# Layer 1's logits, masks and left sums on sixteen 32x32 tiles of TensorE, with the masks loaded per step and row group

## The chip, the cores and the metric

The kernel runs on one core of a Trainium2 chip. The metric is the device time of one execution in microseconds (us). The kernel before takes 3537.9 us (median of three runs, 3537.0 to 3539.0).

## The reference

Two graph layers run one after the other on 4096 nodes with 512 features. Both take the same adjacency matrix `adj` (4096 x 4096), of which under 2% is not zero. Layer 0 is full attention with `adj` added twice to the logits. Layer 1, where the change is, has 8 heads of 64 and masked logits that are a sum of two vectors:

```
h  = relu(layernorm(x));  nX = standardized (h @ W) per head           # 8 x 4096 x 64
kg = at1[:, :, None] + at2[:, None, :]                                 # logits of every pair
kg = leaky_relu(kg, 0.2) * adj
mg = where(adj != 0, kg, -32768);  attention = softmax(mg)
x  = x + elu(attention @ nX + nX)
```

## The kernel before, in words

**Layer 0** runs over 256 tiles of 128 sources by 512 rows. Beside its own work each tile of `adj` leaves two things for layer 1 (`for_layer_1`, L707 to L716): the mask `ng` (bf16, 0 where there is an edge, a large negative number where there is none), stored in the DRAM tensor `nT_d` (L715), and the weights `gs` (f32), stored in `gT_d` (L716).

**Layer 1** has 512 steps, `STEPS`. A step is one chunk of 512 rows (`ic`, 8 of them), one group of four heads (`hg`, 2) and one tile of 128 sources (`jt`, 32). 32 steps with the same rows and heads make a group, so there are 16 groups. Every step passes through these functions, in several steps' distance:

- `left_sums(n+1)` on TensorE writes logits of heads 0 and 2 into the PSUM tile `l` (two buffers). It multiplies `z2` (a source's six bf16 parts for each of four heads, in rows 0, 32, 64 and 96 and after) by `z1_left`, a copy of `z1` in which only heads 0 and 2 are not zero. Four matmuls of 64 x 64 (L1075).
- `left_relu(n+1)` on ScalarE applies relu times four in place (L1081).
- `sums(n)` on TensorE adds, for heads 1 and 3 into the PSUM tiles `r0` and `r1` (one buffer each) and for heads 0 and 2 onto `l`, first the logits (`z_product`, four matmuls with 6 rows and 128 columns, L1065) and then the mask, as a product with the identity (eight matmuls of 64 x 64, L1095). [...]
- `right_leaky(n)` on VectorE (L1113, two instructions) makes heads 1 and 3 out of `r1` and `r0`; `right_weigh(n)` on GpSimd (L1119) multiplies them by `g`; `left_weigh(n)` on VectorE (L1122) multiplies `l` by `g` and so frees its buffer.
- `exponent(n-2)` on ScalarE (L1126) takes all four heads.
- `values(n-4)` on TensorE (L1134, f32) adds attention times values to the PSUM tile `accs`.

The program keeps its written order on every engine (`seq`). The loop at the end of `fast_path` writes it: in step n TensorE gets `sums(n)`, `left_sums(n+1)` and the two halves of `values(n-4)`. All loads are issued by SP, in order. Every fourth step `load_adj` fetches `z2`, `nb`, the two halves of `nx` and `g` for the next four steps (L1009, L1013, L1019, L1024). Each has two buffers. When a group's values are complete, `finish` copies `accs` (ScalarE L1187, VectorE L1188) and spreads the rest over later steps: four turns to rows on TensorE (L1198) with a division on VectorE (L1210, L1211), additions by GpSimd's DMA queue, and the store. At that place `exponent(n-2)` is issued in two halves of two heads, one ahead of the copies and one behind. Before layer 1 starts, SP loads `xns` (L1309): four loads of 256 KB one after the other, one for each group of 32 partitions.

Of the kernel before, what the change touches and what calls it, by code (L numbers as in the profile page):

```python
# [11 lines left out]
BF16 = mybir.dt.bfloat16  # L12
# [67 lines left out]
def fast_path(  # L80
# [67 lines left out]
    nT_d = dram.tile([NB, P, N], BF16, name="nT_d")  # L148
# [177 lines left out]
    with tc.tile_pool(name="rows_in", bufs=2) as rows_in, tc.tile_pool(  # L326
# [357 lines left out]
        with tc.tile_pool(name="turns", bufs=6) as turns, tc.tile_pool(  # L684
# [23 lines left out]
            def for_layer_1(s):  # L708
                ic, jt = TILES[s]
                aT = turned[s] if s >= SB else firsts[s]  # L710
                ng = work.tile([P, GC], BF16, name="ng", tag="ng", bufs=2)
                seq(nc.vector.tensor_scalar(ng, aT, 0.0, NEG_BIG, ALU.is_equal, ALU.mult))
                gs = work.tile([P, GC], F32, name="gs", tag="gs", bufs=2)
                seq(nc.vector.scalar_tensor_tensor(gs, ng, G_MASKED / NEG_BIG, aT, ALU.mult, ALU.add))  # L714
                nc.sync.dma_start(out=nT_d[jt, :, ts(ic, GC)], in_=ng)  # L715
                nc.sync.dma_start(out=gT_d[jt, :, ts(ic, GC)], in_=gs)  # L716
# [271 lines left out]
    with tc.tile_pool(name="ga_g", bufs=2) as adjs, tc.tile_pool(  # L988
# [13 lines left out]
        z1_lefts = [gat.tile([P, GC], BF16, name=f"z1_left{k}") for k in range(2)]  # L1002
        for z in z1_lefts:
            seq(nc.vector.memset(z, 0.0))

        def load_adj(q):
            ic, _, jt = STEPS[q * JB]
            z2 = inputs.tile([P, JB * P], BF16, name="z2", tag="z2", bufs=2)
            seq(nc.sync.dma_start(  # L1009
                out=z2, in_=z2_d[:, STEPS[q * JB][1], jt * P : (jt + JB) * P]  # L1010
            ))
            ng = inputs.tile([P, JB, GC], BF16, name="nb", tag="nb", bufs=2)
            seq(nc.sync.dma_start(  # L1013
                out=ng, in_=nT_d[jt : jt + JB, :, ts(ic, GC)].rearrange("t p i -> p t i")
            ))

            nx = inputs.tile([P, JB, GC], BF16, name="nx", tag="nx", bufs=2)
            for r in range(2):
                seq(nc.sync.dma_start(  # L1019
                    out=nx[ts(r, HD)],  # L1020
                    in_=nT_d[jt : jt + JB, ts(1 - r, HD), ts(ic, GC)].rearrange("t p i -> p t i"),
                ))
            g = adjs.tile([P, JB, GC], F32, name="g", tag="g", bufs=2)
            seq(nc.sync.dma_start(  # L1024
                out=g, in_=gT_d[jt : jt + JB, :, ts(ic, GC)].rearrange("t p i -> p t i")
            ))
            loads[q] = (g, (ng, nx), z2)
# [5 lines left out]
        def open_group(n, queue):  # L1033

            ic, hg, _ = STEPS[n]
            z1_left = z1_lefts[(2 * ic + hg) % 2]
            for first in (0, HD):
                rows = slice(first, first + 6)
                seq(queue.dma_start(out=z1_left[rows, :], in_=z1_d[rows, hg, ts(ic, GC)]))
# [3 lines left out]
            groups[ic, hg] = {"z1": z1, "z1_left": z1_left, "u4": u4}  # L1043
# [17 lines left out]
        def z_product(n, hh, out, start):  # L1061

            ic, hg, jt = STEPS[n]
            rows = slice(32 * hh, 32 * hh + 6)
            seq(nc.tensor.matmul(  # L1065
                out, loads[n // JB][2][rows, ts(jt % JB, P)], groups[ic, hg]["z1"][rows, :],
                start=bool(start), stop=False, skip_group_check=not start,
            ))

        def left_sums(n):  # L1070

            lefts[n] = psum.tile([P, 2, GC], F32, name="l", tag="l", bufs=2)
            ic, hg, jt = STEPS[n]
            for r, c in ((0, 0), (1, 1), (0, 1), (1, 0)):
                seq(nc.tensor.matmul(  # L1075
                    lefts[n][ts(c, HD), r, :], loads[n // JB][2][ts(r, HD), jt % JB * P + c * HD :][:, :HD],
                    groups[ic, hg]["z1_left"][ts(r, HD), :], start=True, stop=True,
                ))
# [4 lines left out]
        def sums(n):  # L1083

            jt = STEPS[n][2]
# [3 lines left out]
            for hh in (1, 3, 0, 2):  # L1089
                z_product(n, hh, out[hh], hh % 2)  # L1090
            masks = loads[n // JB][1]
            for first in (1, 0):
                for r, c in ((0, 0), (1, 1), (0, 1), (1, 0)):
                    rows = ts(r, HD)
                    seq(nc.tensor.matmul(  # L1095
                        out[first + 2 * r][ts(c, HD), :], ident_b[rows, rows],
                        masks[r != c][rows, jt % JB, :], start=False, stop=True,
                        skip_group_check=first == 0,
                    ))
            rights[n] = right  # L1100

        def both_heads(n):
            return loads[n // JB][0][:, STEPS[n][2] % JB, :].unsqueeze(1).to_broadcast([P, 2, GC])
# [390 lines left out]
        at_block(14, load_adj, 0)  # L1494
        for ic in range(2):
            load_normalized(ic)
# [39 lines left out]
        for n in range(n_steps + 4):  # L1536
# [12 lines left out]
            if n % JB == 0 and q < n_steps // JB:  # L1549
                load_adj(q)  # L1550
# [31 lines left out]
            if done and STEPS[n - 4][2] == NB - 1:  # L1582
                if ready:
                    exponent(n - 2, slice(0, 2))
                finish(n, *STEPS[n - 4][:2])
                if ready:
                    exponent(n - 2, slice(2, 4))
# [407 lines left out]
```

## Time and profile before

| | us |
|---|---|
| median of three runs | 3537.9 |
| the profiled execution | 3538.4 |
| its span | 3536.6 |
| TensorE busy in it | 3492.0 |
| GpSimd busy | 2285.6 |
| VectorE busy | 2574.3 |
| ScalarE busy | 1771.1 |
| layer 1's matmuls of the values (L1134), 4096 of 0.605 | 1003.0 (they overlap) |
| ScalarE's exponents (L1126), 527 | 976.5 |
| from one group's start to the next in layer 1 | 98.4 |

The profile is of one execution. "Busy" is the union of an engine's instructions; matmuls overlap, so a busy TensorE isn't one at its peak. The page's line of DMA shares says how much of the time the core's 16 DMA engines were occupied, and the line below it how many GB/s they moved; the two need not go together. The chain of waits is followed back from the last instruction to what released each. A stretch of the profile is given by its start and end in us from the start of the span.

### The profile page before, as it was taken

Reading aid. Unit: us, or ns where it says so; the run is one execution under the profiler, and the core shown is the slowest. Engines: PE = TensorE matmul, PEld = TensorE weight load, DVE = VectorE, ACT = ScalarE, POOL = GpSimd, SP = SyncE. Lnnn points to the kernel's source line nnn. Section 1 sums busy time; section 2 is a strip of 40 time slices with the busy share of each in tenths; the row PEclk is TensorE's granted clock in tenths of the full one; section 3 lists DMA queues with packets and bytes.
Section 4 is the critical chain, followed back from the end, with each engine's and each line's share of the span. In section 5 each row is a group of like instructions: output and inputs, shape, how many; then the busy total and the mean of one; then the engine's idle time right before and its main releaser. Section 6 shows DMA issues by size and latency. Waiting matters only on the chain.

```text
span 3536.6 us, 59808 instructions
## 1 busy us (share of the span) xinstructions
PE 3492.0 (99%) x21898; PEld 2149.6 (61%) x21898; DVE 2574.3 (73%) x4262; ACT 1771.1 (50%) x1580; POOL 2285.6 (65%) x1863
## 2 busy tenths in 40 slices
PE   9999999999999999999999999999999999999998
PEld 7888888888888888888887223223222323232232
DVE  6765665656565666656567888888888888888887
ACT  2100111111111111111133999999999999999997
POOL 6754444444444444444567888788888888888886
PEclk9999999999999999999999999999999999999999
DMA  6688888888888888888768777787778877777885
GB/s 226 219 247 246 233 232 250 234 244 247 235 246 247 231 252 241 237 248 232 235 135 183 210 207 204 205 208 214 211 209 219 214 215 206 198 209 209 214 213 147
DMA packets 633550, 779.07 MB, mean 220 GB/s; under 512 B 78560, under 2 KB 461216, under 8 KB 624032
## 3 DMA queue, kind: packets, MB, share of 16 engines
q1 hardware_dynamic: 615680, 742.34, 73.5%
q0 software_dynamic: 16464, 31.98, 5.3%
q8 instruction: 174, 2.85, 0.3%
q10 hardware_dynamic: 1104, 0.85, 0.1%
q14 instruction: 128, 1.05, 0.1%
HBM read 592.97 MB, written 174.19 MB: 217 GB/s over the span
## 4 chain that ended last, share of the span: by engine, by line
PE 90%; DVE 7%; ACT 1%; DMA 1%; issue 1%; SPq 0%; DVEq 0%; ACTq 0%
PE accs L1134 25%; PE XZ L722 21%; PE M L777 20%; PE r L1095 4%; PE r L1065 4%; PE l L1075 3%; PE X L508 3%; PE l L1095 3%; PE Z L508 2%; DVE t L1122 2%; PE y L1327 1%; PE pt L1198 1%; DVE x L837 1%; DVE y L1211 1%; PE accs L1327 1%
## 5 line engine op out<-in xcount | busy, mean ns | idle before, releaser
L1119 POOL TENSOR_TENSOR t<-t,g 128x1024 f32<-128x1024 f32 x512 | 1225.6, 2406 | 268.9 <-DVE t L1113 233.3
L1134 PE MATMUL accs<-t,nX 128*64 128x512 f32 x4096 | 1003.0, 605 | 4.6 <-DVE ob L1188 4.6
L1126 ACT ACTIVATE t<-t 128x2048 f32<-128x2048 f32 (+1 forms) x527 | 976.5, 1853 | 0.2 <-POOL t L1119 0.2
L1113 DVE SCALAR_TENSOR_TENSOR t<-u,at2m,r 128x512 f32<-128x512 f32 x1024 | 719.3, 744 | 194.2 <-issue 152.0
L738 ACT ACTIVATE aT<-aT 128x512 f32<-128x512 f32 x256 | 161.2, 630 | 1387.3 <-DVE aT L734 1387.3
L734 DVE TENSOR_TENSOR aT<-aT,XZ 128x256 f32<-128x256 f32 x884 | 348.7, 418 | 575.1 <-PE XZ L722 570.8
L1122 DVE TENSOR_TENSOR t<-l,g 128x1024 f32<-128x1024 f32 x512 | 623.4, 1218 | 0.0
L1081 ACT ACTIVATE l<-l 128x1024 f32<-128x1024 f32 x512 | 516.3, 1008 | 117.5 <-PE l L1075 66.2
L1134 PEld LDWEIGHTS accs<-t,nX 128*64 128x64 f32 x4096 | 246.5, 136 | 461.9 <-issue 449.5
L722 PE MATMUL XZ<-qt,hS 128*128 128x256 f32 x2024 | 479.1, 379 | 1.0
L750 POOL TENSOR_TENSOR S<-aT 128x256 f32<-128x256 f32 x128 | 93.5, 731 | 506.9 <-ACT aT L738 506.9
L722 PEld LDWEIGHTS XZ<-qt,hS 128*128 128x128 f32 x2024 | 383.9, 190 | 55.9 <-DVE aT L734 4.0
L722 PE MATMUL XZ<-qt,hT 128*128 128x256 f32 x1520 | 369.5, 379 | 0.0
L762 POOL TENSOR_TENSOR total<-total,aT 128x256 f32<-128x256 f32 x360 | 323.0, 910 | 9.4
L722 PEld LDWEIGHTS XZ<-qt,hT 128*128 128x128 f32 x1520 | 288.8, 190 | 39.3
L1065 PEld LDWEIGHTS <-z 6*128 6x128 bf16 x2048 | 52.4, 91 | 422.2 <-DVE t L1113 353.8
L751 POOL TENSOR_TENSOR aT<-aT 128x256 f32<-128x256 f32 x128 | 93.6, 731 | 284.1 <-ACT aT L738 284.0
L777 PE MATMUL M<-tv,aT 128*128 128x256 f32 x1024 | 262.6, 379 | 0.0
L777 PE MATMUL M<-v,aT 128*128 128x256 f32 x1024 | 262.6, 379 | 0.0
L777 PE MATMUL M<-v,S 128*128 128x256 f32 x1024 | 242.5, 380 | 0.0
L714 DVE SCALAR_TENSOR_TENSOR gs<-ng,aT 128x512 f32<-128x512 bf16 x252 | 222.7, 884 | 8.7
L777 PEld LDWEIGHTS M<-v,aT 128*128 128x128 f32 x1024 | 194.6, 190 | 26.5
(267 smaller groups left out, 4552.4 us busy)
## 6 DMA issues: line engine op xcount, KB each, us to landing
g<-gT_d SPq DMA_DIRECT2D x128, 1024.0 KB
ag<-in_adj_dram SPq DMA_DIRECT2D x256, 256.0 KB
hS<-s_d SPq DMA_DIRECT2D x64, 1024.0 KB
gT_d<-gs SPq DMA_DIRECT2D x256, 256.0 KB
nb<-nT_d SPq DMA_DIRECT2D x128, 512.0 KB
nx<-nT_d SPq DMA_DIRECT2D x256, 256.0 KB
hT<-h_d SPq DMA_DIRECT2D x64, 768.0 KB
tv<-vt_d SPq DMA_DIRECT2D x128, 384.0 KB
```

The costliest lines, as they stand in the source:

```text
L714: seq(nc.vector.scalar_tensor_tensor(gs, ng, G_MASKED / NEG_BIG, aT, ALU.mult, ALU.add))
L722: seq(nc.tensor.matmul(out, a, b, start=start and k == 0, stop=k == 1, skip_group_check=not start,))
L734: seq(nc.vector.tensor_add(p, before, part))
L762: seq(nc.gpsimd.tensor_add(t, t, a))
L777: seq(nc.tensor.matmul(sums[ic][i][:, u, :], a[:, ts(u, P)], b, start=jt == 0 and u == 0, stop=jt == NB - 2, skip_group_check=u == 1,))
L1081: seq(nc.scalar.activation(lefts[n], lefts[n], AF.Relu, scale=4.0))
L1095: seq(nc.tensor.matmul(out[first + 2 * r][ts(c, HD), :], ident_b[rows, rows], masks[r != c][rows, jt % JB, :], start=False, stop=True, ski ...
L1113: seq(nc.vector.scalar_tensor_tensor(t[:, 2 + e, :], u4[:, e, :], at2m[:, jt, h : h + 1], right[e], ALU.max, ALU.add))
L1119: seq(nc.gpsimd.tensor_mul(t[:, 2:4, :], t[:, 2:4, :], both_heads(n)))
L1122: seq(nc.vector.tensor_mul(logits[n][:, 0:2, :], lefts.pop(n), both_heads(n)))
L1126: seq(nc.scalar.activation(t, t, AF.Exp))
L1134: seq(nc.tensor.matmul(accs[ts(e, HD), hf, :], nX[jt // SB][:, jt % SB, hg * HG + 2 * hf + e, :], t[:, hf + 2 * e, :], start=jt == 0, stop ...
```

## The change

The masks of a tile are stored in another order, 32 source rows to a block. A step's masks are then loaded into a tile of their own, three steps ahead: four loads, each of the same 128 KB, one into each group of 32 partitions. So each of the four heads has all 128 sources of the mask on its own 32 partitions. `nb` (now with four buffers of one step), `nx` and `z1_left` in their old form are gone. Logits, masks and left sums are written as 32-column matmuls, four to a head: 16 logits, 16 masks and 8 left sums per step. `load_g` is split off and runs one step later than `load_adj`. At a group's end the copies come first and the exponent follows whole.

```diff
-    nT_d = dram.tile([NB, P, N], BF16, name="nT_d")
+    nT_d = dram.tile([NB, NI, R, SB, GC], BF16, name="nT_d")
...
-                nc.sync.dma_start(out=nT_d[jt, :, ts(ic, GC)], in_=ng)
+                nc.sync.dma_start(out=nT_d[jt, ic].rearrange("p c i -> c p i"), in_=ng)
...
-        z1_lefts = [gat.tile([P, GC], BF16, name=f"z1_left{k}") for k in range(2)]
-        for z in z1_lefts:
-            seq(nc.vector.memset(z, 0.0))
...
-            ng = inputs.tile([P, JB, GC], BF16, name="nb", tag="nb", bufs=2)
...
-            nx = inputs.tile([P, JB, GC], BF16, name="nx", tag="nx", bufs=2)
...
+            loads[q] = {"z2": z2}
+
+        def load_g(q):
+            ic, _, jt = STEPS[q * JB]
             g = adjs.tile([P, JB, GC], F32, name="g", tag="g", bufs=2)
...
+        def load_masks(n):
+
+            ic, _, jt = STEPS[n]
+            masks[n] = inputs.tile([P, SB, GC], BF16, name="nb", tag="nb", bufs=4)
+            for r in range(SB):
+                seq(nc.sync.dma_start(out=masks[n][ts(r, R)], in_=nT_d[jt, ic]))
...
+        def z_products(n, hh, out, **flags):
 
             ic, hg, jt = STEPS[n]
-            rows = slice(32 * hh, 32 * hh + 6)
...
+            rows = slice(R * hh, R * hh + 6)
+            for c in range(SB):
+                seq(nc.tensor.matmul(
+                    out[ts(c, R), :], loads[n // JB]["z2"][rows, jt % JB * P + c * R :][:, :R],
+                    groups[ic, hg]["z1"][rows, :], **flags,
+                ))
 
         def left_sums(n):
 
             lefts[n] = psum.tile([P, 2, GC], F32, name="l", tag="l", bufs=2)
...
+            for r in range(2):
+                z_products(n, 2 * r, lefts[n][:, r, :], start=True, stop=True)
...
+            order = (1, 3, 0, 2)
+            for hh in order:
+                right_one = hh % 2 == 1
+                z_products(n, hh, out[hh], start=right_one, stop=False, skip_group_check=not right_one)
+            for hh in order:
+                rows = ts(hh, R)
+                for c in range(SB):
                     seq(nc.tensor.matmul(
-                        out[first + 2 * r][ts(c, HD), :], ident_b[rows, rows],
-                        masks[r != c][rows, jt % JB, :], start=False, stop=True,
-                        skip_group_check=first == 0,
+                        out[hh][ts(c, R), :], ident_b[rows, rows], masks[n][rows, c, :],
+                        start=False, stop=True, skip_group_check=hh % 2 == 0,
                     ))
...
         at_block(14, load_adj, 0)
+        at_block(14, load_g, 0)
+        for n in range(3):
+            at_block(14, load_masks, n)
...
-            if n % JB == 0 and q < n_steps // JB:
-                load_adj(q)
+            if n + 3 < n_steps:
+                load_masks(n + 3)
+            if n % JB < 2 and q < n_steps // JB:
+                (load_adj, load_g)[n % JB](q)
...
             if done and STEPS[n - 4][2] == NB - 1:
-                if ready:
-                    exponent(n - 2, slice(0, 2))
                 finish(n, *STEPS[n - 4][:2])
                 if ready:
-                    exponent(n - 2, slice(2, 4))
+                    exponent(n - 2)
```

More of the change, by code (lines that the diff above doesn't have):

```diff
@@ L1011, in load_adj @@
             ))
-            ng = inputs.tile([P, JB, GC], BF16, name="nb", tag="nb", bufs=2)
-            seq(nc.sync.dma_start(
-                out=ng, in_=nT_d[jt : jt + JB, :, ts(ic, GC)].rearrange("t p i -> p t i")
-            ))
-            nx = inputs.tile([P, JB, GC], BF16, name="nx", tag="nx", bufs=2)
[L1018 to L1022, printed above, removed]
+            loads[q] = {"z2": z2}
+        def load_g(q):
+            ic, _, jt = STEPS[q * JB]
             g = adjs.tile([P, JB, GC], F32, name="g", tag="g", bufs=2)
@@ L1026, in load_adj @@
             ))
-            loads[q] = (g, (ng, nx), z2)
+            loads[q]["g"] = g
+        masks = {}
+        def load_masks(n):
[3 more added lines that the diff above has]
+                seq(nc.sync.dma_start(out=masks[n][ts(r, R)], in_=nT_d[jt, ic]))
         def cols(ic, hg):
@@ L1035, in open_group @@
             ic, hg, _ = STEPS[n]
[L1036 to L1039, printed above, removed]
             z1 = inputs.tile([P, GC], BF16, name="z1", tag="z1", bufs=2)
@@ L1042, in open_group @@
             u4 = inputs.tile([P, 2, GC], F32, name="u4", tag="u4", bufs=2)
-            groups[ic, hg] = {"z1": z1, "z1_left": z1_left, "u4": u4}
+            groups[ic, hg] = {"z1": z1, "u4": u4}
             load_u4(n, 0, queue)
@@ L1059, in fast_path @@
         lefts, rights = {}, {}
-        def z_product(n, hh, out, start):
+        def z_products(n, hh, out, **flags):
             ic, hg, jt = STEPS[n]
-            rows = slice(32 * hh, 32 * hh + 6)
[L1065 to L1068, printed above, removed]
+            rows = slice(R * hh, R * hh + 6)
[4 more added lines that the diff above has]
+                ))
         def left_sums(n):
             lefts[n] = psum.tile([P, 2, GC], F32, name="l", tag="l", bufs=2)
[L1073 to L1078, printed above, removed]
+            for r in range(2):
+                z_products(n, 2 * r, lefts[n][:, r, :], start=True, stop=True)
         def left_relu(n):
@@ L1083, in sums @@
         def sums(n):
-            jt = STEPS[n][2]
             left = lefts[n]
@@ L1088, in sums @@
             out = [left[:, 0, :], right[0], left[:, 1, :], right[1]]
[L1089 to L1094, printed above, removed]
+            order = (1, 3, 0, 2)
[5 more added lines that the diff above has]
+                for c in range(SB):
                     seq(nc.tensor.matmul(
-                        out[first + 2 * r][ts(c, HD), :], ident_b[rows, rows],
-                        masks[r != c][rows, jt % JB, :], start=False, stop=True,
-                        skip_group_check=first == 0,
+                        out[hh][ts(c, R), :], ident_b[rows, rows], masks[n][rows, c, :],
+                        start=False, stop=True, skip_group_check=hh % 2 == 0,
                     ))
+            masks.pop(n)
             rights[n] = right
         def both_heads(n):
-            return loads[n // JB][0][:, STEPS[n][2] % JB, :].unsqueeze(1).to_broadcast([P, 2, GC])
+            return loads[n // JB]["g"][:, STEPS[n][2] % JB, :].unsqueeze(1).to_broadcast([P, 2, GC])
         def right_leaky(n):
```

## The prediction

> **What bounds the kernel now.** I read the profiled execution's page first (its span, the busy shares, the slices), then the stretches by stage, then the timeline and the chain of waits inside one step of layer 1, and last the DMA queues.
>
> ```profile
> span 3536.6 us, 59808 instructions
> PE 3492.0 (99%) x21898; PEld 2149.6 (61%) x21898; DVE 2574.3 (73%) x4262; ACT 1771.1 (50%) x1580; POOL 2285.6 (65%) x1863
> ```
>
> TensorE is busy from end to end. The time of this execution is 3538.4 us, 1.8 us around its span, and 0.5 us over the median of 3537.9, so sums against 3538.4 may be read against the median.
>
> The change lives in layer 1, the last 1600 us. The next view is the TensorE timeline of one step of it (start, duration, line).
>
> ```profile
> 2601.89 0.39 PE L1065 MATMUL r<-z,z 6*128 6x512 bf16 x2
> 2602.22 0.40 PE L1095 MATMUL r<-nb,ident_b 64*64 64x512 bf16 x2
> 2602.46 0.38 PE L1095 MATMUL l<-nb,ident_b 64*64 64x512 bf16 x2
> 2602.68 0.39 PE L1075 MATMUL l<-z_left,z 64*64 64x512 bf16 x4
> 2602.99 1.94 PE L1134 MATMUL accs<-t,nX 128*64 128x512 f32 x8
> 2604.86 0.39 PE L1065 MATMUL r<-z,z 6*128 6x512 bf16 x2
> ```
>
> Start to start: logits 0.33, masks 0.24 and 0.22, left sums 0.31, values 1.87, together 2.97 us. The chain of waits in this stretch is TensorE alone, so an ordinary step is bound by TensorE. From the trace, 32 steps (a group) repeat every 98.4 us, 3.075 a step: 27 ordinary ones of 2.967 and five at the group's end (3.79, three of 3.74, 3.29). In those three the chain runs DVE left_weigh L1122, left sums, half the values, the turn to rows L1198, the division L1211, left_weigh again; no logit or mask stands in it.
>
> The second candidate is the DMA queue.
>
> ```profile
> core 0: us, PE busy (x) PEld busy (x) DVE busy (x) ACT busy (x) POOL busy (x), PEclk, DMA share, GB/s
> 2604.50:2606.30 1.80, 1.80 (x20) 0.56 (x20) 1.35 (x2) 1.66 (x2) 1.80 (x1) 1.00 0.98 310
> 2606.50:2607.60 1.10, 1.10 (x8) 0.23 (x4) 1.10 (x3) 1.10 (x2) 0.41 (x2) 1.00 1.08 205
> 2611.70:2613.20 1.50, 1.50 (x14) 0.48 (x8) 1.50 (x3) 1.36 (x3) 0.94 (x1) 1.00 1.04 363
> 1778.50:1784.00 5.50, 5.50 (x27) 4.85 (x26) 1.50 (x4) 0.63 (x1) 0.84 (x2) 1.00 1.06 247
> ```
>
> Here the last two columns count. All four stretches have full DMA engines, and yet the rate differs by what lands: 310 GB/s for the 128-partition mask load nb, 205 for the 64-partition halves nx, 363 for transfers over 128 partitions (g and what follows it), and 247 at 1778.5 for the xns loads, which go to 32 partitions each, in 2 KB pieces, four row groups in turn. Full engines with few partitions move less.
>
> **The change, part by part.**
>
> *TensorE.* Logits, masks and left sums go from 4, 8 and 4 matmuls on three array shapes to 16, 16 and 8 on one shape. No 32x32 tile is in the trace; the nearest row is four 64x64 tiles at once (matmuls 3 to 4 ns apart, next batch 0.22 us later, 0.24 after a change of shape). If sixteen tiles run as four do: logits 0.24, masks 0.22 in one batch, left sums and the change of shape 0.31, some 0.05 for the longer stagger, values 1.87: 2.69 us, 0.28 less. If nothing overlapped better than now it would gain 0. I take 0.28.
>
> *What is late next.* The left sums of step n+2 overwrite the buffer that left_weigh of step n reads. Today that leaves 0.3 us of air. After: the right masks start 0.24 us into the step, take 0.03 to issue, and VectorE starts 0.54 after that (now: masks 2605.19, DVE 2605.76, 0.57); L1113 twice 1.32, L1122 1.22, 0.05 to TensorE: 3.40 after the step's start. From the left sums to the next step is 0.31 + 1.87 + 0.03. Two steps make this round, so (3.40 + 2.21) / 2 = **2.80** us. ScalarE needs 0.92 + 1.80 = 2.72 (starts of L1081 to L1126 and, when nothing is awaited, back) and hides. So the engines' side allows 2.967 - 2.80 = 0.167 us in 27 x 16 = 432 steps: 72 us. The five steps at a group's end keep their chain.
>
> *The masks' DMA.* Removed per four steps: nb 512 KB and nx 2 x 256 KB. Added per step: 4 x 128 KB, each to 32 partitions. 262 KB a step become 524 KB, because every row group gets the whole step's masks. The bounds on 524 KB come from the rows above: at 363 GB/s 1.44 us, at 205 GB/s 2.56 us. I take the xns row, nearest in shape (32 partitions, four row groups in turn, SP queue): 524 / 247 = **2.12** us. The rest of a step's transfers: g 262 KB at 354 (mean of the better rows) 0.74; z2 33 KB 0.11; outputs, z1 and u4 37 KB 0.12. The POOL queue has 9.1% of the engines in layer 1:
>
> ```profile
> q1 hardware_dynamic: 223632, 270.69, 68.9%
> q0 software_dynamic: 11424, 22.02, 9.1%
> ```
>
> 0.091 x 3.075 = 0.28 a step; its packets may fill gaps of the other queue, so 0 to 0.28, taken at 0.14. Sum 2.12 + 0.74 + 0.11 + 0.12 + 0.14 = **3.23** us a step, above 2.80 and above today's mean of 3.075. The sum for today by the same rows (131 KB at 310, 131 KB at 205 in place of the 2.12) is 0.42 + 0.64 + 1.11 = 2.17, 71% of 3.075, against a share of 78% in the profile: it doesn't overstate. Masks are fetched three steps ahead, which hides latency but not a lack of rate; the slow steps at a group's end are in the 3.075 already. So 512 x (3.23 - 3.075) = **+79 us**. The ends: 1.44 and no POOL share give 2.41, which hides under 2.80 (-72 us); 2.56 and all of it give 3.81 (+376).
>
> [...]
>
> *SP.* It issues 18 loads in four steps in place of five. Eight xns loads took 4.77 us to issue, 0.60 each, in a full queue: 4.5 x 0.60 = 2.7 us a step, just under 2.80; it is hidden under 3.23, and if the DMA were faster it would be close to showing. load_g moves a step back, where its buffer is free: now SP waits some 2 us before issuing g (nx ends 2604.7, g 2606.74). With a transfer queue that is full this hides nothing.
>
> *The store of the masks, layer 0.* 256 stores of 128 KB keep their bytes and 1 KB pieces, but the destination is now four blocks of 32 rows. In the trace a load of 6 rows (z_left) lands with 7 semaphore updates where the others have 16, so a transfer is spread by its rows. If the new store were spread by its 4 blocks, four engines would carry 32 pieces each in place of 8: 24 more of 46 ns (a 1 KB packet in the trace) per tile of 7.1 us, 0.16 on top of a DMA share of 0.84. That is just full; 2% over would be 36 us of layer 0's 1800. I take 0, with 36 as the other end: TensorE's loads are there two tiles ahead.
> [...]
>
> *Group's end.* The copy of accs now stands ahead of an exponent that was cut in two. Now the first half (1.05 us) fills ScalarE's wait for the last values and the copy starts as they end; after, ScalarE waits and runs one of 1.90, later by 0.9 us. Its next left relu is then ready before TensorE, which waits here for VectorE's copy anyway. 0 us; 16 x 0.9 = 14 us if that cover is gone. The two memsets and the 32 small z_left loads go: nothing on the path.
>
> **The forecast and its rivals.** Forecast: layer 1 is bound by DMA, 3538 + 79 = about **3615 us**, slower. Chance 0.54.
>
> *Rival 1, faster: the mask loads keep up.* If two row groups that use different parts of SBUF overlap, 524 KB take less than 1.7 us and the ring of left_weigh and left sums decides: 3538 - 72 = 3466 us. For it: single slices of 0.3 us in the xns stretch reach 313 GB/s, and 128 KB loads change the row group twice as often as xns. Against: no stretch of the page's 88 us moves over 252 GB/s, and 2.80 us a step needs (524 + 262 + 33 + 37 + 48) KB / 2.80 = 323. Between the two, when the masks run at about 270 GB/s, gains of 10 to 60 us. It decides for slower once a step's transfers take over 3.075 us. Chance 0.36.
>
> *Rival 2, no change:* the two meet at 3.06 to 3.09 a step, within 0.2% (7 us), which is about what a measurement can tell from no change. Chance 0.06.
>
> *Rival 3, TensorE can't be fed.* A step has 80 + 16 weight loads and matmuls in place of 48 (one per 62 ns). The densest 64 in a row of the trace take 3.0 us (3520.6), 47 ns each. Were that a floor, a step would be 4.5 us and layer 1 670 us longer. That row waits for copies in its middle, and queued ones start 2 to 4 ns apart, so I give it 0.04; the store's 36 us alone are counted in the range.
>
> Faster by over 0.2% 0.36, within 0.2% 0.06, slower 0.58. The range 3460 to 3760 takes in rival 1 whole and a mask rate down to 220 GB/s with half the POOL share (2.38 + 1.11 = 3.49, +212, 3750); what is left out, 205 GB/s or rival 3, I hold at less than 0.15.
>
> **What would show it.** Right: in layer 1 the DMA share near 1 in nearly all slices, the masks' matmuls waiting for DMA, steps of about 3.2 us, the chain of waits passing through nb. TensorE's five parts should take 2.69 us where nothing is awaited. Wrong: slices with DMA share under 0.9 and steps of 2.80 with TensorE waiting for DVE's left_weigh (rival 1), or gaps between neighbouring matmuls of one batch (rival 3). Layer 0's end, now about 1800 us, should not move.

## The result and the profile after

The changed kernel takes 3875.8 us (median of six runs, 3864.2 to 3883.9), against 3538.4 for the kernel before on the same chip (six runs): a ratio of 1.095, 95% interval 1.0934 to 1.0967. It is 337 us slower. The forecast was 3615 us, the range 3460 to 3760: the direction and the bound were right, the size was not. The profiled execution has a span of 3874.1 us.

The page of the changed kernel, its busy shares and its slices (the span in 40 slices of 97 us, each digit the busy share in tenths; the last twenty slices are layer 1 with the last 20 us of its preparation):

```profile
PE 3573.9 (92%) x34186; PEld 2176.7 (56%) x34186; DVE 2580.9 (67%) x4260; ACT 1766.8 (46%) x1565; POOL 2273.9 (59%) x1863
...
PE   9999999999999999999988888888888888888887
...
PEclk9999999999999999999989999889999999998998
DMA  6588888888888888886789999999999999999997
GB/s 231 208 247 232 235 239 241 241 240 243 240 242 241 243 235 238 235 230 173 182 209 240 251 241 249 244 239 244 252 246 243 251 244 253 244 249 238 251 247 196
```

In the kernel before TensorE was at nine tenths or more in all but the last slice; here it no longer is in layer 1. The DMA engines are at nine tenths or more in nearly every slice there, and move 238 to 253 GB/s (the last slice aside). The highest slice of the kernel before moved 252.

Two stretches of layer 1, first of the kernel before, then of the changed one. The last three columns are the granted clock, the DMA share and GB/s.

```profile
2300.00:2600.00 300.00, 297.56 (x2444) 89.28 (x2440) 255.60 (x320) 278.82 (x204) 248.04 (x114) 1.00 0.79 211
2600.00:2900.00 300.00, 297.46 (x2436) 89.21 (x2432) 256.23 (x321) 278.80 (x205) 245.67 (x114) 1.00 0.78 212
```

```profile
2300.00:2600.00 300.00, 260.65 (x4002) 79.77 (x4001) 214.52 (x270) 232.01 (x168) 203.46 (x93) 0.93 0.99 245
2600.00:2900.00 300.00, 259.06 (x3930) 78.00 (x3931) 210.71 (x260) 228.13 (x165) 203.89 (x94) 0.91 0.99 247
```

The DMA share went from 0.79 to 0.99, and TensorE, VectorE, ScalarE and GpSimd all lost 12 to 18% of their busy time: none of them is the bound. The chain of waits of the changed kernel between 2800 and 2850 us (start, length, what) shows what they wait for. First comes a group's end as before, then this:

```profile
2815.85 0.44 SPq L1025
2816.29 0.04 issue
2816.34 8.23 DMA nb<-nT_d
2824.63 1.39 SPq L1025
2826.03 0.04 issue
2826.07 0.42 SPq L1025
2826.49 0.04 issue
2826.53 6.10 DMA nb<-nT_d
2832.65 8.41 DMA nb<-nT_d
```

L1025 is the mask load. In these 50 us 69% of the chain is mask loads on their way. Over the whole execution the chain is 36% DMA, where it was 1%.

Where the 337 us are: the first step of layer 1 starts at 1957.3 us in place of 1935.3 (layer 0's last tile, L777, ends 16.1 us later, the preparation of layer 1 takes 5.9 more; here and below the end of layer 0 is told by the start of its last matmul); the 511 step starts that follow are 3.703 us apart in place of 3.085, 316 us.

But a step that waits for nothing is faster than before. The TensorE timeline of two steps of the changed kernel (L1060 logits and left sums, L1086 masks, L1125 values):

```profile
2802.45 0.41 PE L1060 MATMUL r<-z,z 6*32 6x512 bf16 x8
...
2803.15 0.41 PE L1060 MATMUL l<-z,z 6*32 6x512 bf16 x8
2803.49 1.94 PE L1125 MATMUL accs<-t,nX 128*64 128x512 f32 x8
2805.36 0.41 PE L1060 MATMUL r<-z,z 6*32 6x512 bf16 x8
2805.39 0.41 PE L1060 MATMUL l<-z,z 6*32 6x512 bf16 x8
2805.59 0.40 PE L1086 MATMUL r<-nb,ident_b 32*32 32x512 bf16 x8
2805.61 0.40 PE L1086 MATMUL l<-nb,ident_b 32*32 32x512 bf16 x8
2805.83 0.40 PE L1060 MATMUL l<-z,z 6*32 6x512 bf16 x8
```

Start to start, logits 0.23 and masks 0.24 (2805.36, 2805.59, 2805.83), left sums 0.34 and values 1.87 (2803.15, 2803.49, 2805.36, in the step before): 2.68. The fastest steps of the execution (its fifth percentile) take 2.668 us. Sixteen small tiles do run as one batch (they start 2 to 5 ns apart and take 0.40 to 0.41 us each); TensorE gained all that was hoped, and then stood still for masks.

The time that DMA packets took between 2300 and 3300 us, added up by queue and size, divided by 16 engines and by the number of steps:

| us a step | before | changed | sliding window, spread (last experiment) |
|---|---|---|---|
| 4 KB packets (masks) | | 2.11 (263 ns each) | 1.51 (188 ns each) |
| 1 KB packets (masks before; z2, z1, out) | 1.19 | 0.20 | 0.16 |
| 2 KB packets (g) | 0.85 | 0.85 | 0.76 |
| 512 B packets (u4) | 0.07 | 0.10 | 0.08 |
| GpSimd's queue | 0.29 | 0.26 | 0.30 |
| 4 B (semaphores), instructions | 0.03 | 0.10 | 0.06 |
| sum | 2.43 | 3.63 | 2.86 |
| a step takes | 3.085 | 3.703 | 2.991 |

### The profile page after: what moved, and what is told of

It reads as the page before. It is cut to its first block, busy times and chain, and to the rows that moved or that the text cites. A ratio compares the mean times of both kernels' runs of the same rounds, so it can differ in the third digit from the quotient of the medians.

```text
span 3874.1 us, 86113 instructions
## 1 busy us (share of the span) xinstructions
PE 3573.9 (92%) x34186; PEld 2176.7 (56%) x34186; DVE 2580.9 (67%) x4260; ACT 1766.8 (46%) x1565; POOL 2273.9 (59%) x1863
## 4 chain that ended last, share of the span: by engine, by line
PE 51%; DMA 36%; SPq 6%; DVE 5%; issue 1%; POOL 0%; ACT 0%; DVEq 0%; POOLq 0%; ACTq 0%
DMA nb<-nT_d 26%; PE XZ L722 16%; PE M L777 16%; PE accs L1125 7%; SPq L1025 4%; DMA tv<-vt_d 4%; PE X L508 3%; PE Z L508 2%; DMA g<-gT_d 2%; DMA z<-z_d 2%; DVE t L1113 1%; PE l L1060 1%; PE y L1318 1%; DMA u<-u_d 1%; PE r L1086 1%
## 5 line engine op out<-in xcount | busy, mean ns | idle before, releaser
L1125 PE MATMUL accs<-t,nX 128*64 128x512 f32 x4096 | 1102.5, 658 | 7.3 <-DVE ob L1179 7.3
L1117 ACT ACTIVATE t<-t 128x2048 f32<-128x2048 f32 x512 | 973.3, 1901 | 3.7 <-POOL t L1110 3.6
L1125 PEld LDWEIGHTS accs<-t,nX 128*64 128x64 f32 x4096 | 262.1, 144 | 462.2 <-issue 449.3
L1060 PEld LDWEIGHTS <-z 6*32 6x32 bf16 x12288 | 166.7, 88 | 619.9 <-DVE t L1104 296.7
L1060 PE MATMUL l<-z,z 6*32 6x512 bf16 x8192 | 435.7, 401 | 40.5 <-DVE t L1113 23.0
L1086 PE MATMUL r<-nb,ident_b 32*32 32x512 bf16 x4096 | 272.0, 397 | 208.4 <-DMA nb<-nT_d 207.5
L762 POOL TENSOR_TENSOR total<-total,aT 128x256 f32<-128x256 f32 x360 | 313.7, 884 | 9.4
L777 PE MATMUL M<-v,aT 128*128 128x256 f32 x1024 | 262.6, 379 | 0.0
L777 PE MATMUL M<-tv,aT 128*128 128x256 f32 x1024 | 262.6, 379 | 0.0
L1086 PEld LDWEIGHTS <-ident_b 32*32 32x32 bf16 x8192 | 92.9, 88 | 284.5 <-issue 283.4
```

Source lines behind the costliest of these rows:

```text
L762: seq(nc.gpsimd.tensor_add(t, t, a))
L777: seq(nc.tensor.matmul(sums[ic][i][:, u, :], a[:, ts(u, P)], b, start=jt == 0 and u == 0, stop=jt == NB - 2, skip_group_check=u == 1,))
L1060: seq(nc.tensor.matmul(out[ts(c, R), :], loads[n // JB]["z2"][rows, jt % JB * P + c * R :][:, :R], groups[ic, hg]["z1"][rows, :], **flags,))
L1086: seq(nc.tensor.matmul(out[hh][ts(c, R), :], ident_b[rows, rows], masks[n][rows, c, :], start=False, stop=True, skip_group_check=hh % 2 == ...
L1117: seq(nc.scalar.activation(t, t, AF.Exp))
L1125: seq(nc.tensor.matmul(accs[ts(e, HD), hf, :], nX[jt // SB][:, jt % SB, hg * HG + 2 * hf + e, :], t[:, hf + 2 * e, :], start=jt == 0, stop ...
```

## The experiments

Fourteen kernels. The first five ask what the cause is, the next two what TensorE's and the group's-end parts of the change do alone, three what happened to layer 0, and four whether the change's gain on the engines can be had without its price in transfers. Times stand beside runs of the kernel before on the same chip (3538.8 to 3539.3 us); ratios are to it, with their 95% intervals.

### One light load a step

```diff
-            for r in range(SB):
-                seq(nc.sync.dma_start(out=masks[n][ts(r, R)], in_=nT_d[jt, ic]))
+            seq(nc.sync.dma_start(out=masks[n][:, 0, :], in_=nT_d[jt, :, ts(ic, GC)]))
...
-                        out[hh][ts(c, R), :], ident_b[rows, rows], masks[n][rows, c, :],
+                        out[hh][ts(c, R), :], ident_b[rows, rows], masks[n][rows, 0, :],
```

> The changed kernel, but with the masks stored as before the change and one load of 128 KB per step over all 128 partitions; all four column groups of a head read that one tile, so three quarters of the mask's columns are left out (the masks' values are not the right ones). TensorE's work, the loop and all other transfers are as in the changed kernel. Theory D (the masks' four loads fill the DMA engines): the transfers fall to about 0.42 + 1.55 = 2.0 us a step, under what the engines need, so an ordinary step takes 2.67 us (its cleanest bursts in the changed kernel) to 2.80 us (the ring of left_weigh and left sums that the prediction worked out), a group 27 x 2.67 + 18.3 = 90 to 27 x 2.80 + 18.3 = 94 us, and the time is 3410 to 3470 us, at a DMA share of 0.7 to 0.8 in layer 1. Rival C (the small tiles on TensorE or the new order of the work are at fault): steps stay at 3.1 us or more, 3540 to 3870 us, with the masks still waiting though the DMA engines have air.

Measured: 3459.4 us, 0.9776 (0.9756 to 0.9795); steps of 2.936 us on average. A stretch of it, with the granted clock, the DMA share and GB/s at the end:

```profile
2300.00:2600.00 300.00, 291.75 (x5038) 96.22 (x5038) 268.41 (x336) 288.34 (x212) 257.14 (x118) 1.00 0.62 177
```

Theory D holds, the small tiles are not at fault. Its DMA share was expected at 0.7 to 0.8: all packets took 1.82 us a step and not 2.0. Ordinary steps in the second half of a group alternate between 2.78 and 2.80 us, and two timelines of this kernel, TensorE and VectorE, show what sets them:

```profile
2868.19 0.41 PE L1059 MATMUL r<-z,z 6*32 6x512 bf16 x8
2868.22 0.41 PE L1059 MATMUL l<-z,z 6*32 6x512 bf16 x8
2868.42 0.40 PE L1085 MATMUL r<-nb,ident_b 32*32 32x512 bf16 x8
2868.44 0.40 PE L1085 MATMUL l<-nb,ident_b 32*32 32x512 bf16 x8
2868.77 0.41 PE L1059 MATMUL l<-z,z 6*32 6x512 bf16 x8
```

```profile
2866.18 1.41 DVE L1103 SCALAR_TENSOR_TENSOR t<-u,at2m,r 128x512 f32<-128x512 f32 x2 [0.25 <-issue]
2867.50 1.22 DVE L1112 TENSOR_TENSOR t<-l,g 128x1024 f32<-128x1024 f32 x1
```

left_weigh (L1112) ends at 2867.50 + 1.22 = 2868.72, and the left sums, which overwrite what it reads, start 0.05 later, at 2868.77, 0.35 after the masks and not 0.24. That is the ring of the prediction.

### The kernel before with the new loads

The matmuls of the kernel before, with the changed kernel's store, `load_masks` and `load_g`:

```diff
-                        masks[r != c][rows, jt % JB, :], start=False, stop=True,
+                        masks[n][rows, r, :], start=False, stop=True,
```

> The kernel before, with its own matmuls, but with the changed kernel's store and its four mask loads per step (its masks read the tiles by row and column of the old scheme, so the masks' values are not the right ones; nothing else is left out). Theory D: the loads alone cost the time, an ordinary step has no slack for them: about 3.7 us a step, 3850 to 3890 us. Rival C (the new matmuls are at fault): steps stay at 2.97 us, 3540 to 3560 us.

Measured: 3912.6 us of two runs, 3885.9 and 3939.3, 1.106 (1.097 to 1.114); steps of 3.724 us, at the loads' pace though half of them still take the old 2.967. The two runs lie 1.4% apart, the one with the profile (3885.9) inside Theory D's 3850 to 3890. Its stretches look like the changed kernel's:

```profile
2600.00:2900.00 300.00, 268.51 (x2027) 77.97 (x2024) 214.52 (x264) 234.18 (x172) 207.10 (x97) 0.96 0.99 251
```

The loads, with their store, cost the time alone, with either form of TensorE's work.

### The same loads, six steps ahead

```diff
-            masks[n] = inputs.tile([P, SB, GC], BF16, name="nb", tag="nb", bufs=4)
+            k = n % 7
+            if k < 5:
+                masks[n] = inputs.tile([P, SB, GC], BF16, name="nb", tag="nb", bufs=5)
+            else:
+                if not more:
+                    more.append(prep.tile([P, 2, SB, GC], BF16, name="nb2", tag="x1", bufs=1))
+                masks[n] = more[0][:, k - 5]
...
-            if n + 3 < n_steps:
-                load_masks(n + 3)
+            if n + 6 < n_steps:
+                load_masks(n + 6)
```

> The changed kernel with seven mask buffers in place of four, so that a step's four 32-partition loads are issued six steps ahead in place of three; nothing else. Theory D (the engines' time on the 32-partition loads is the limit, DMA share 0.98): 3.65 to 3.70 us a step, 3850 to 3880 us. Theory L (the lead is what made the sliding-window kernel faster): 3.1 to 3.3 us a step, 3570 to 3670 us.

Measured: 3875.8 us, 1.0951 (1.0929 to 1.0973), steps of 3.702 us. Twice the lead changes nothing (3.703 with three steps): it is the rate of the engines, not latency.

### The order of the row groups

```diff
-            for r in range(SB):
+            for r in (0, 2, 1, 3):
```

> The changed kernel with a step's four mask loads issued for the row groups in the order 0, 2, 1, 3 in place of 0, 1, 2, 3. Theory D1 (the engines' rate into 32 partitions is what it is, whichever 32): no change, 3876 us within 10. [...]

Measured: 3802.3 us, 1.0744 (1.0726 to 1.0762): 74 us faster than the changed kernel. Packets of 4 KB fell from a mean of 263 to 233 ns (fifth percentile 159), the masks to 1.89 us a step (277 GB/s), the DMA share to 0.95. D1 falls: it matters which row groups follow each other. But a mean of 233 ns is still well over the 159, and what the rest of the price is this run doesn't show.

### Pieces of 1 KB

```diff
-                seq(nc.sync.dma_start(out=masks[n][ts(r, R)], in_=nT_d[jt, ic]))
+                seq(nc.sync.dma_start(out=masks[n][ts(r, R)], in_=nT_d[jt, :, ts(ic, GC)].rearrange("(c p) i -> p c i", p=R)))
```

with the store as before the change.

> The changed kernel with the masks stored in DRAM as before the change (128 rows of 4096); the four loads of a step then fetch the same bytes to the same partitions in pieces of 1 KB in place of 4 KB. For layer 0: the store goes over 16 engines again, so its last tile should end at about 1791 us in place of 1807 if the store on four engines cost those 16 us; at 1807 if something else did. For layer 1: theory D, bytes into 32 partitions set the price: 3.70 us a step as in the changed kernel, time 3855 us. If pieces have a price of their own (1 KB packets of 46 ns elsewhere, four of them 184 ns, against 263 ns for one of 4 KB now) the mask time could move either way: 2.1 x 184 / 263 = 1.5 us would give some 3.1 us a step and 3550 us; 2.1 x 1.3 would give 4.3 and 4180.

Measured: 4000.6 us, 1.1304 (1.128 to 1.1327). Layer 0 ends at 1791.7 us again, but a step takes 3.98. All 1 KB packets together take 2.68 us a step, 75 ns each, four of them 302. Nine in ten are masks; the rest (z2, z1 and the output) took 0.20 in the changed kernel, which leaves the masks some 2.48 against 2.11 in 4 KB packets. Theory D's 3855 us falls: pieces have a price of their own. The new store costs layer 0 some 15 us and saves layer 1 140: storing the masks in 4 KB pieces was right.

### Small logits, old masks

The kernel before with `z_products` and `left_sums` of the changed one, and its own loads and 64x64 masks.

> The kernel before with logits and left sums on 32x32 tiles as in the change, and the masks as before the change: 64x64 matmuls, loads nb and nx, one store of 128 rows. z1_left and its loads go. Theory D and the prediction's TensorE step: logits fall from 0.33 to 0.24 us, masks and left sums stay, an ordinary step falls from 2.97 to about 2.88 us, 0.09 x 432 = 39 us less: 3500 us. If small tiles gained nothing: 3538. If the change of array shape between 32x32 and 64x64 cost more than one batch (0.1 us or more, twice a step): 3560 to 3580.

Measured: 3607.7 us, 1.0197 (1.0182 to 1.0213); 3.127 us an ordinary step, 0.16 more than before. It is the third case, and worse than its bound. The timeline of one step:

```profile
2796.00 0.41 PE L1058 MATMUL r<-z,z 6*32 6x512 bf16 x8
...
2796.37 0.40 PE L1084 MATMUL r<-nb,ident_b 64*64 64x512 bf16 x2
...
2796.61 0.38 PE L1084 MATMUL l<-nb,ident_b 64*64 64x512 bf16 x2
...
2796.92 0.41 PE L1058 MATMUL l<-z,z 6*32 6x512 bf16 x8
2797.26 1.94 PE L1123 MATMUL accs<-t,nX 128*64 128x512 f32 x8
```

Logits to masks takes 0.37 us (0.23 where the shape stays 32x32, in the view of the changed kernel), masks to left sums 0.31 (0.24). These two runs put 0.14 and 0.07 us on the two changes of shape. The gain of the change is in keeping one shape for all three; half of it is a loss, 0.16 us a step here.

### The group's end alone

The kernel before with the copies first and the exponent whole.

```diff
-                if ready:
-                    exponent(n - 2, slice(0, 2))
                 finish(n, *STEPS[n - 4][:2])
                 if ready:
-                    exponent(n - 2, slice(2, 4))
+                    exponent(n - 2)
```

> The kernel before with only the end of a group changed: the copies of accs first, then the exponent whole. The prediction's step: 0 us, because TensorE waits there for VectorE's copy; the other end 16 x 0.9 = 14 us slower, 3552 us, if ScalarE's relu then comes late.

Measured: 3538.7 us, ratio 1.0000 (0.9991 to 1.0009), groups of 98.4 us. Nothing, as expected.

### Layer 0's store

The load order 0, 2, 1, 3 and, in place of the one store with four blocks outermost:

```diff
+                for c in range(SB):
+                    nc.sync.dma_start(out=nT_d[jt, ic, :, c, :], in_=ng[ts(c, R)])
```

> The changed kernel with the load order 0, 2, 1, 3 and the masks' store as four DMAs of 32 rows, one for each block, in place of one with four blocks outermost. If the one store's spread over four engines cost layer 0's 16 to 22 us, its last tile ends at about 1791 us in place of 1807, and the time is 3802 - 16 to 22 = 3780 to 3786 us. If the block order in DRAM or the number of stores costs it, 3802 or more.

Measured: 3812.2 us, 1.0778 (1.0761 to 1.0794). Layer 0's last tile ends at 1802.6 us, 4 us earlier than with one store, not 16; layer 1's steps (3.586 us) are a little longer than in the run it is compared with (3.563). The next run is the kernel before with four stores into the old layout:

```diff
-                nc.sync.dma_start(out=nT_d[jt, :, ts(ic, GC)], in_=ng)
+                for c in range(SB):
+                    nc.sync.dma_start(out=nT_d[jt, ts(c, R), ts(ic, GC)], in_=ng[ts(c, R)])
```

> The kernel before with only the masks' store changed: four DMAs of 32 rows each into the same place in the old layout. In the changed kernel (one store with four blocks outermost) layer 0's last tile ended at 1806.9 us and with four stores of 32 rows into the new layout at 1802.6, against 1790.8 before the change and 1791.7 with the changed loads but the old store. If stores that take 32 partitions at a time, or the three more issues, are the cost: the last tile ends near 1803 us and the time is about 3550. If the new order of the rows in DRAM is: 1791 us, 3538.

Measured: 3551.7 us, 1.0031 (1.0019 to 1.0043), layer 0's end at 1803.0: 12 us, with the old order in DRAM. So four stores of 32 partitions cost 12 us by themselves, and one store of four blocks 16. To tell the issues from the partitions, the four stores were given to ScalarE, in the sliding-window kernel of the next section that loads g by step:

```diff
-                    nc.sync.dma_start(out=nT_d[ic, jt, :, c, :], in_=ng[ts(c, R)])
+                    nc.scalar.dma_start(out=nT_d[ic, jt, :, c, :], in_=ng[ts(c, R)])
```

> The same, with layer 0's four mask stores issued by ScalarE in place of SP. If SP's three more issues a tile are what makes layer 0 end 12 to 14 us later, the last tile ends near 1791 us and the time is 12 us under that of the run beside it. If the stores' 32 partitions are the cost (1 KB packets of 54 ns in place of 47.5), no change.

Measured: 3678.2 us, 1.0392 (1.0375 to 1.0409). It doesn't answer the question: layer 0 ends at 1898.8 us. ScalarE's waits between 300 and 1750 us that ended with one of its stores (us in total, times, longest):

```profile
ACT aT L739 <- DMA nT_d<-ng: 776.4, 139, 9.9
```

Another 458 us of its waits end with VectorE. In the run beside it ScalarE waited 1270 us for VectorE in the same stretch, and layer 0 ended at 1803.0. So it doesn't wait longer in all; what makes up the 96 us isn't shown.

### Four row groups in one load: the sliding window

A load of 128 partitions brings row group h the tile of step m + h: four neighbouring tiles, which lie one behind the other in DRAM when the masks are stored by `ic` and then `jt`. Step n reads row group h from load n - h. The bytes and the pieces of 4 KB stay. Four stores of 32 rows write them.

```diff
-            for r in range(SB):
-                seq(nc.sync.dma_start(out=masks[n][ts(r, R)], in_=nT_d[jt, ic]))
...
+            masks[m] = inputs.tile([P, SB, GC], BF16, name="nb", tag="nb", bufs=5)
+            h = 0
+            while h < SB:
+                n, k = m + h, 1
+                if 0 <= n < n_steps:
+                    ic, _, jt = STEPS[n]
+                    while h + k < SB and jt + k < NB:
+                        k += 1
+                    seq(nc.sync.dma_start(
+                        out=masks[m][h * R : (h + k) * R],
+                        in_=nT_d[ic, jt : jt + k].rearrange("t p c i -> (t p) c i"),
+                    ))
+                h += k
...
-                        out[hh][ts(c, R), :], ident_b[rows, rows], masks[n][rows, c, :],
+                        out[hh][ts(c, R), :], ident_b[rows, rows], masks[n - hh][rows, c, :],
...
+            if n + 2 < n_steps:
+                load_masks(n + 2)
```

> The changed kernel's whole computation and the same 524 KB of masks a step in the same pieces of 4 KB, but each load covers 128 partitions: row group h takes the tile of step m + h, so that one load brings four row groups the tiles of four neighbouring steps, and step n reads the last four loads. The masks' store is four DMAs of 32 rows. Theory D (the price is that of 32 partitions at a time): the load runs at the 310 to 363 GB/s that 128-partition loads showed in the kernel before, 1.44 to 1.69 us a step in place of 2.11; with 1.42 (what the other transfers took in the run with light masks) to 1.55 us for the rest, 2.86 to 3.24 us a step against 2.94 that the run with light masks needed: 3459 to 3615 us, most likely about 3490. Rival B (the bytes alone set the price, wherever they land): 2.11 + 1.55 = 3.66 us a step, about 3850 us.

Measured: 3792.2 us, 1.0719 (1.0699 to 1.0738), outside what D said, and not what B said. The masks took 1.62 us a step on the engines (200 ns a packet, median 159), inside D's 1.44 to 1.69, and the DMA share fell to 0.83; but a step took 3.539 us. SP's own waits in this run between 2300 and 3300 us:

```profile
SPq L1031 <- PE l L1070: 361.7, 116, 10.7
SPq L1031 <- PE r L1096: 212.0, 84, 3.3
SPq L1031 <- PE l L1096: 201.6, 85, 9.6
```

SP holds the next mask load back (L1031) until TensorE has used a buffer: with five buffers, three of them history, the lead is two steps. D's first half (the engines' price) held; the time was lost to a wait that this kernel brought in. The window also makes one load out of four, so it doesn't part the price of 32 partitions from that of more and smaller loads; the order 0, 2, 1, 3, with the same four loads, shows that the partitions have some part in it (263 to 233 ns a packet). With seven buffers, two of them in a tile that layer 0 no longer needs, it becomes four:

```diff
-            if n + 2 < n_steps:
-                load_masks(n + 2)
+            if n + 4 < n_steps:
+                load_masks(n + 4)
```

> The sliding-window kernel with seven mask buffers in place of five (two of them lie in space that layer 0 leaves free), so that a load is issued four steps before its step and not two. In the run with five buffers the masks took 1.62 us a step on the DMA engines, all transfers together 2.94, and the engines were busy 0.83 of the time, yet TensorE stopped up to 10 us at a time for a mask. Theory L (the rest of the loss was the short lead: one load late behind the 1 MB load of g, the next not issued until TensorE moved on): the stops go, the step falls to 2.94 to 3.05 us on average, the time to 3475 to 3530 us. Theory D alone (the DMA engines have no more to give): the time stays near 3790 us, and the DMA share stays near 0.83 with the stops in place.

Measured: 3575.5 us, 1.0105 (1.0088 to 1.0122): 217 us less, 3.119 us a step, at 0.93 of the engines and 288 to 294 GB/s. Theory L holds for most of it; 3475 to 3530 was too low. Then g in four quarters, one a step:

```diff
+        def load_g(q, j):
+            ic, _, jt = STEPS[q * JB]
+            if j == 0:
+                loads[q]["g"] = adjs.tile([P, JB, GC], F32, name="g", tag="g", bufs=2)
+            seq(nc.sync.dma_start(out=loads[q]["g"][:, j, :], in_=gT_d[jt + j, :, ts(ic, GC)]))
```

> The sliding-window kernel with a lead of four steps, and g loaded step by step (256 KB, three steps ahead, behind the step's masks) in place of 1 MB every fourth step, which SP had to hold back until GpSimd gave its buffer free (108 us of SP's waits in 1000 us) with up to three mask loads piled up behind it. Theory L (what is left of layer 1's loss, 3.12 us a step against 2.94 with light masks, is queueing behind g): the step falls to 2.95 to 3.02 us and the time to 3490 to 3525 us. Theory D (the DMA engines, busy 0.93 of the time, are the limit): 3555 to 3580 us, with a DMA share near 0.93 still.

Measured: 3574.8 us, 1.0102 (1.0082 to 1.0122). No gain: loading 1 MB of g at once was not what was left. The time and the share (0.91 to 0.94) are those of Theory D. But 22 of a group's 32 steps now take under 3.0 us on average, and one, the next to last, 6.41 (mean of the fifteen groups that another follows). The stretches around such a stop (2844.6 to 2853.3), with the columns as above:

```profile
2812.00:2818.00 6.00, 6.00 (x100) 1.93 (x98) 5.50 (x8) 6.00 (x6) 6.00 (x5) 1.00 1.00 267
...
2830.00:2836.00 6.00, 5.32 (x96) 1.56 (x64) 5.29 (x7) 5.60 (x5) 5.05 (x3) 1.00 1.04 392
...
2842.00:2848.00 6.00, 3.69 (x80) 1.05 (x49) 1.83 (x4) 3.65 (x3) 1.74 (x2) 0.93 1.05 208
2848.00:2854.00 6.00, 4.84 (x48) 1.27 (x53) 3.64 (x4) 2.82 (x2) 4.62 (x2) 0.50 1.00 358
```

From 2812 on the engines are full but for 2836 to 2842 (0.89), and TensorE stops 30 us later: z1 and u4 of the next group (2820.9, 2821.4, 2834.6), the output's store (2830.7) and the windows' part loads at the turn of the group come one after the other. What comes too late at the stop is not a mask but a quarter of g: VectorE's left_weigh (L1127) and GpSimd wait for it, and the left sums (L1074) for left_weigh. The waits between 2840 and 2856 us (us in total, times, longest):

```profile
POOL t L1124 <- DMA g<-gT_d: 4.3, 1, 4.3
DVE t L1127 <- DMA g<-gT_d: 3.9, 1, 3.9
PE l L1074 <- DVE t L1127: 3.4, 1, 3.4
```

After the wait the granted clock is 0.50 for 6.8 us, and the values of that step take 3.68 us in place of 1.94. The last run moves z1 and u4 away:

```diff
-            if n + 10 < n_steps and STEPS[n + 10][2] == 0:
-                open_group(n + 10, nc.sync)
-            if n + 6 < n_steps and STEPS[n + 6][2] == 0:
-                load_u4(n + 6, 1, nc.sync)
+            if n + 24 < n_steps and STEPS[n + 24][2] == 0:
+                open_group(n + 24, nc.sync)
+            if n + 17 < n_steps and STEPS[n + 17][2] == 0:
+                load_u4(n + 17, 1, nc.sync)
```

> The sliding-window kernel with lead four and g by step, and the next group's z1 and u4 loaded 24 and 17 steps ahead in place of 10 and 6, away from the stretch in which the output's store and the windows' part loads come. Theory B (the burst ahead of a group's end is what is left): the one stop of 6 to 9 us in each of 16 groups shrinks by half or more, 50 to 80 us less: 3495 to 3525 us. Theory D (the DMA rate is the limit throughout: 2.90 us of transfers a step against 2.94 that the engines need): the stop moves to another place, 3560 to 3580 us.

Measured: 3509.8 us (3496.9 to 3517.7), 0.9907 (0.988 to 0.9934). Theory B holds: the next to last step of a group falls from 6.41 to 3.28 us. So the engines' rate, Theory D, was not the limit throughout. This version is faster than both kernels: 29 us under the one before, 366 under the changed one. Its stretches:

```profile
2300.00:2600.00 300.00, 287.86 (x4944) 94.76 (x4942) 263.75 (x330) 283.58 (x208) 253.73 (x119) 1.00 0.96 307
2600.00:2900.00 300.00, 286.37 (x4900) 94.21 (x4900) 262.46 (x329) 283.13 (x208) 252.88 (x117) 1.00 0.95 307
```

307 GB/s where the changed kernel moved 246, with the same bytes a step and a granted clock of 1.00 again. Its steps take 2.991 us on average, the run with light masks 2.936; of the 55 us between their profiled executions (3514.5 and 3459.5), 25 are the later start of layer 1, layer 0's store among them (its first step is at 1957.4 us, that of the light masks at 1932.4), and 512 x 0.055 = 28 the steps.

## Why the prediction was right in direction and wrong in size

*TensorE, 2.97 to 2.69 us.* Right: 2.67.

*What is late next, the ring of 2.80 us, 72 us in all.* Right: 2.78 and 2.80 in the run with light masks, which is 80 us faster than the kernel before. In the changed kernel the ring came to bear in some steps only. In 214 of 511 the left sums come at least 0.03 us later than the masks would let them, within 0.1 us of left_weigh's end (as at 2803.15 in the view above, where left_weigh ends at 2803.10), 62 us in all; the freest steps ran down to 2.67. It was not the bound.

*The masks' DMA, 524 / 247 = 2.12 us.* Right: 2.11, 248 GB/s. That it fits so well is in part luck, since the xns row has 2 KB pieces and the masks 4 KB, and the size of the pieces counts: with 1 KB the masks took some 2.48. Turning the order to 0, 2, 1, 3 raised the 248 to 277, so part of the price is paid between neighbours in the queue. The 220 GB/s at the slow end of the range are the author's choice, and no run shows them: the masks' loads to 32 partitions ran at 248 and 277 in pieces of 4 KB and by an estimate at 524 / 2.48 = 211 in pieces of 1 KB, and the stretch of the kernel before with the 64-partition loads of nx (the mask with its halves swapped) moved 205.

*The rest of a step's transfers, 0.74 + 0.11 + 0.12 + 0.14 = 1.11 us.* **This is the step that failed.** Measured by the packets' times: g 0.85 and not 0.74; z2, outputs, z1 and u4 0.30 and not 0.23; GpSimd's queue 0.26 and not 0.14; semaphore packets and instructions 0.10, which were not in the sum (74.3 packets of 4 B a step, with 18 loads in four steps, where the kernel before had 22.5); and 0.07 idle. Together 1.58. With the masks 3.69, against 3.70 measured. Of the 261 us between forecast and measurement, about 512 x 0.47 = 241 are this step and 22 the later start of layer 1. Two choices made it: g was priced at "the mean of the better rows", though g's own 2 KB packets took 0.85 us a step in the kernel before as well, and POOL's share was halved on the hope that it fills gaps. At a share of 0.98 there were hardly any gaps to fill: that queue's packets still took 0.26. And the test that the prediction made of itself was read the wrong way round: the sum for the kernel before gave 2.17 us where its trace has 0.787 x 3.085 = 2.43. That it "doesn't overstate" was taken for comfort; it was a shortfall of 0.26 that belongs on top. With it the step would have been 3.49 and the time some 3750 us, inside the range. What was missing then, 0.21, is known in part: against the kernel before, semaphores and instructions took 0.07 more, u4's 512 B packets 0.03 more, GpSimd's queue 0.03 less, and 0.07 were idle. The other 0.07 lies in the 1 KB packets of the kernel before, which the trace doesn't part into masks and others.

*No long stretch over 252 GB/s.* The prediction used this only against rival 1. Taken as the rate itself, 904 KB a step at 252 GB/s are 3.59 us, nearer than the sum.

*SP, 0.60 us a load, hidden.* Held in the main: 4.6% of the chain between 2800 and 2850 us is SP's issue, 6% over the whole. SP itself mostly waits for earlier loads to land, which points to a full queue as the reason: between 2300 and 3300 us its mask loads waited 228 us for loads of g and 84 us for other mask loads.

*The store of the masks, 0 with 36 us as the other end.* Wrong value, right bounds: layer 0 ended 16 us later. "Layer 0's end should not move" fell with it. The new store's 1 KB packets do run fewer at a time: between 300 and 1750 us, where the masks' stores alone have packets of this size, four at most were under way in 462 of the 515 us in which any was, in the kernel before in 120 of 240. The new store lands with 5 semaphore updates where the old one had 16, the last a median of 6.0 us after the start of its issue in place of 4.1. But four stores that land with 16 updates each cost 12 us too. Whether that is their 32 partitions (1 KB packets of 54 ns in place of 47.5) or the three more issues stays open.

*The group's end, 0.* Right: 1.0000.

*The rivals.* Rival 1's engine side was right and its condition failed: 323 GB/s were needed and 246 came. It was close to being the case for another kernel: 307 GB/s brought 3510 us. Rival 3 fell: the 32x32 tiles of a batch issue 2 to 5 ns apart. The preparation of layer 1, which the prediction left out, took 150.0 us in place of 144.1. With the light masks it took 142.7; in the other kernels with 524 KB of masks a step 145.1 to 150.5, the sliding windows among them. What makes the difference stays open.

## What to carry to other kernels

When a change moves the bound to the DMA engines, add up what packets of each queue and size took in the trace of the kernel at hand, not bytes at its better rates, and put on top whatever that sum lacks of the measured share (0.26 us a step here). A copy that is wanted on every group of 32 partitions was cheaper here as one load over all 128, with neighbouring data for neighbouring groups, than as four loads of 32 (1.62 us a step on the engines and not 2.11); it cost buffers, and with five of them the gain turned into a wait (3.539 us a step, and 3.119 with seven). And with the transfers at 0.91 to 0.94 of the time, it counted when a group's odd transfers were issued: moving z1 and u4 alone brought 65 us.

## What the runs showed of the hardware

- A 4 KB packet to 32 partitions took 263 ns on average in a full queue and 233 with the row groups in the order 0, 2, 1, 3; in loads over 128 partitions 188 to 200, with a median of 159, close to the least of all of them (156).
- With loads to 32 partitions in 1 KB pieces, four 1 KB packets took 302 ns on average (all of this size, nine in ten of them masks), where one of 4 KB took 263.
- A change of the array's shape between 32x32 and 64x64 cost 0.14 us (32x32 to 64x64) and 0.07 us (back), against batches of 0.23.
- The granted clock fell to 0.91 to 0.93 in layer 1 of the changed kernel, where TensorE waits, and to 0.50 in the 6 us around the end of one stop; it was 1.00 where TensorE was fed. In that stop it cost time: the values took 3.68 us in place of 1.94. What it cost in the changed kernel, with the DMA engines at 0.97 to 0.99, no run shows.
- With four stores a tile issued by ScalarE, 776 us of ScalarE's waits (in 1450 us) ended with one of these stores, and layer 0 ended 96 us later than with SP issuing them.
